# A mixture-of-experts decoder layer: routed products weighted and scattered to token order by each tile, instead of gathered per token at the end

## The chip, the cores and the metric

The kernel runs on one core of a Trainium2 chip. The metric is device time in microseconds, from the first to the last instruction of the core and the little that lies around it; the time of a kernel is the median of its runs. One further execution is taken with the hardware profiler; every line of a profile shown here comes from that execution.

## The reference, cut to what matters

The input is 64 sequences of 128 tokens with 256 channels, float32, 8,192 tokens in all. Each token passes a state-space block, a cross attention, and then this feed-forward block with a residual and a layernorm around it:

```python
shared = (silu(x @ shared_gate.T) * (x @ shared_up.T)) @ shared_down.T
probs = sigmoid(x @ router_w.T + routing_bias)          # 8 experts
scores, indices = top_k(probs, 2)
scores = scores / sum(scores)
w = zeros(tokens, 8); w[token, indices] += scores
g = silu(einsum('th,ehi->tei', x, gate_w))
u = einsum('th,ehi->tei', x, up_w)
combined = einsum('tei,eih,te->th', g * u, down_w, w)
out = layernorm(x + shared + combined)
```

Only the two experts with a weight other than zero need to be computed for a token. So there are 16,384 rows to send through an expert, each 256 floats (1 KB).

## The kernel before, in words

All of it lies in `_shared_decay`. Tokens are handled in `NG` = 16 groups of `GB` = 4 sequences (512 tokens). A group goes through `front`, `scan`, `after` (state space, attention, layernorm; its result is `x2`), then `route`, and then its shared expert, `shared`.

**Routing.** `route` ranks the experts of each token, finds by a prefix sum the row that each of the token's two copies gets in its expert's region of the DRAM array `xs`, writes that row into `index`, and sends the rows of `x2` there with 8 indirect DMAs on POOL (L1024). Then it works out `weight`, the two scores of each token, and keeps it in SBUF.

**Tiles.** `tile_list(k)` turns the counts of the experts into a list of tiles. There are five batches (`BATCHES`): 57 tiles of 256 rows and, in the last batch, 21 of 128 rows. In the last batch the rows behind the end of each expert are filled with zeros (8 indirect DMAs, L1096). `routed` runs over the tiles. `fetch` copies the tile's entry on POOL (L1196), and SP reads it into registers, loads the expert's weights (1.5 MB into one of `NW` = 3 slots, L1199, which waits until the last user of the slot is done) and the rows (L1205, into `rows_in`, 3 buffers). `hidden` transposes the rows on PE (L1219) and makes the gate and up products, ACT applies silu, DVE multiplies. `down` makes the down product, ACT copies it to `rows_out` (2 buffers, L1245), and SP stores it to the DRAM array `ys` in tile order (L1246). The tile loop runs `down(i-1)` after `hidden(i)`, and then fetches ahead.

**The end.** `places` (80 small DVE instructions) changes every entry of `index` from a row of `xs` to a row of `ys`. For the groups 7 to 13 (`LATE`), `x2` has been parked in the DRAM array `x2_rows`, and their shared expert is computed only now (`late_shared`, L1337), interleaved with `combine` of all 16 groups. `combine` gathers the two products of each token from `ys` with 8 indirect DMAs on POOL (`picked`, 12 buffers of 1 KB per partition, L1268), adds them with the weight as a scalar (8 DVE instructions, L1272), makes the layernorm and stores the group. In `layernorm` POOL computes `rstd` (L636), DVE then `shift` (L638), and ACT applies both (L641). `load_rows` (L1074) brings `x2` or `x2` plus shared product back into `x2_back`, 4 buffers.

**What sets the order.** `weave` interleaves generators by shares: in the stage after the groups, `places` along the remaining tiles; at the end, `combine` along `late_shared`. The framework then fixes the queue of each engine before the run, and each engine works its queue strictly in order. A place in the weave is a priority rather than a position. So the 16 steps of `places` were meant for the length of 180 steps of tiles, but the trace has their first and last multiply-compare (L1168) start at 1565.8 and 1614.0 us.

Of the kernel before, what the change touches and what calls it, by code (L numbers as in the profile page):

```python
# [16 lines left out]
P = 128  # L17
# [25 lines left out]
NR = sum(n * r for _, _, n, r in BATCHES)  # L43
# [463 lines left out]
def _shared_decay(ctx, K):  # L507
# [84 lines left out]
    index = const.tile([P, NG * GB, 2], mybir.dt.int32, name="index")  # L592
    weight = const.tile([P, NG * GB, 2], F32, name="weight")

    x2_rows = dram.tile([NG, P, GB * D], F32, name="x2_rows", bufs=1)
    xs = dram.tile([NE * CAP + (NE - 1) * P, D], F32, name="xs", bufs=1)
    ys = dram.tile([NR, D], F32, name="ys", bufs=1)
# [13 lines left out]
    bounds = const.tile([P, NE, len(BATCHES)], F32, name="bounds")  # L611
    moves = const.tile([P, NE, len(BATCHES)], F32, name="moves")
    known = [0]
    weights = []
    for i in range(NW):
# [3 lines left out]
    zeros = const.tile([P, D], F32, name="zeros")  # L619
    nc.vector.memset(zeros, 0.0)  # L620
    nc.sync.dma_start(
        out=xs[NE * CAP :, :].rearrange("(i p) d -> p i d", p=P),
        in_=zeros.unsqueeze(1).to_broadcast([P, NE - 1, D]),
    )
# [227 lines left out]
    def after(g, st):  # L852
# [69 lines left out]
        x2 = ring.tile([P, GB, D], F32, name="x2", bufs=2)  # L922
# [10 lines left out]
        st["x2"] = x2  # L933

    writers = []

    def wrote(g, ins):

        tc.declare_no_dep(ins, group="scatters", reason="other rows")
        for k, (groups, *_) in enumerate(BATCHES):  # L940
            if groups <= g:
                tc.declare_no_dep(ins, group=f"fetches{k}", reason="other rows")
        for group in ("scatters", f"scatters{g}"):
            tc.add_to_no_dep_group(group, ins)
        writers.append((g, ins.name))

    def read(k, ins):

        tc.add_to_no_dep_group(f"fetches{k}", ins)
        for g in range(BATCHES[k][0], NG):  # L950
            tc.declare_no_dep(ins, group=f"scatters{g}", reason="other rows")
        for g, name in writers:
            if g < BATCHES[k][0]:
# [10 lines left out]
    def route(g, st):  # L964
# [44 lines left out]
        here = slice(g * GB, (g + 1) * GB)  # L1009
# [11 lines left out]
        nc.vector.tensor_copy(index[:, here, :], at)  # L1021
        for b in range(GB):
            for k in range(2):
                s = nc.gpsimd.indirect_dma_start(  # L1024
                    out=xs, in_=x2[:, b, :], in_offset=None,
                    out_offset=bass.IndirectOffsetOnAxis(ap=index[:, g * GB + b, k : k + 1], axis=0),
                )
                wrote(g, s.ins)
        yield
# [6 lines left out]
        nc.vector.tensor_tensor(  # L1036
            weight[:, here, :], wk2, tot.unsqueeze(2).to_broadcast([P, GB, 2]), ALU.mult
        )
        if g in LATE:
            nc.sync.dma_start(out=x2_rows[g], in_=x2.rearrange("p b d -> p (b d)"))  # L1040
# [33 lines left out]
    def load_rows(g):  # L1074
        t = late.tile([P, GB, D], F32, name="x2_back", bufs=4)
# [3 lines left out]
    def tile_list(k):  # L1079
# [5 lines left out]
        base = sum(m * r for _, _, m, r in BATCHES[:k])  # L1085
# [3 lines left out]
        if last:  # L1089

            behind = small.tile([P, NE], F32, name="behind", bufs=1)
            nc.vector.tensor_tensor(behind, pn, behind0, ALU.add)
            behind_i = small.tile([P, NE], mybir.dt.int32, name="behind_i", bufs=1)
            nc.vector.tensor_copy(behind_i, behind)
            for e in range(NE):
                s = nc.gpsimd.indirect_dma_start(  # L1096
                    out=xs, in_=zeros, in_offset=None,
                    out_offset=bass.IndirectOffsetOnAxis(ap=behind_i[:, e : e + 1], axis=0),
                )
                wrote(groups - 1, s.ins)  # L1100
# [18 lines left out]

        lo = bounds[:, :, k]  # L1120
        nc.vector.tensor_tensor(lo, d, begin1, ALU.add)
        nc.vector.tensor_scalar(cum2[:, 0, :], cum0, float(size), float(base), ALU.mult, ALU.add)
        nc.vector.tensor_tensor(moves[:, :, k], cum2[:, 0, :], lo, ALU.subtract)
# [30 lines left out]
    def places():  # L1154

        n = NE * len(BATCHES)
        step = small.tile([P, n], F32, name="step", bufs=1)
        flat = moves.rearrange("p e k -> p (e k)")
        nc.vector.tensor_copy(step[:, 0:1], flat[:, 0:1])
        nc.vector.tensor_tensor(step[:, 1:], flat[:, 1:], flat[:, 0 : n - 1], ALU.subtract)  # L1160
        low = bounds.rearrange("p e k -> p (e k)")
        for g in range(NG):
            here = slice(g * GB, (g + 1) * GB)
            m = GB * 2
            was = small.tile([P, m], F32, name="was", bufs=1)
            nc.vector.tensor_copy(was, index[:, here, :].rearrange("p b k -> p (b k)"))
            over = small.tile([P, m, n], F32, name="over", bufs=1)
            nc.vector.tensor_tensor(  # L1168
                over, was.unsqueeze(2).to_broadcast([P, m, n]), low.unsqueeze(1).to_broadcast([P, m, n]), ALU.is_ge
            )  # L1170
            nc.vector.tensor_tensor(over, over, step.unsqueeze(1).to_broadcast([P, m, n]), ALU.mult)
            by = small.tile([P, m], F32, name="by", bufs=1)
            nc.vector.tensor_reduce(by, over, AX.X, ALU.add)
            nc.vector.tensor_tensor(
                index[:, here, :].rearrange("p b k -> p (b k)"), was, by, ALU.add
            )
            yield

    def routed():
# [3 lines left out]
        def shape(i):  # L1183

            row = 0
            for k, (_, first, n, size) in enumerate(BATCHES):
# [344 lines left out]
```

## Time and profile before

| | before |
|---|---|
| time, median of 3 runs (lowest, highest) | 2177.42 us (2176.56, 2180.04) |
| the profiled execution: time, span | 2202.88 us, 2201.2 us |
| PE busy | 1986.6 us, 90% |
| DVE, ACT, POOL busy | 1043.9, 733.6, 433.9 us (47%, 33%, 20%) |
| mean granted TensorE clock | 0.959 |
| moved by DMA | 244.85 MB, 111 GB/s |

The time has four parts. Up to about 60 us the first data come in. Up to about 1560 us the groups pass through, with the first tiles among them. Up to 1947 us the remaining tiles run, and from then on the late shared experts and the sums. The profiled execution is 1.2% longer than the median of the plain runs, so differences within the trace are read against 2202.88 and carried over to 2177.42.

In a list of waits a line names the engine and instruction that waited, after the arrow what ended the wait, and then the total, the count and the longest in us. In a timeline a line has the start and length in us, the engine, the line of the code, and in brackets how long the engine had been idle before. SPq is the queue of SP, from which DMAs are issued. PE records of float32 matmuls come in pairs, so 32 records are 16 matmuls.

### The profile page before, as it was taken

To read this page: it belongs to the slowest core of one execution; us is meant where nothing else is said; L and a number is where in the kernel's file an instruction comes from. 1 tells how busy PE (TensorE), PEld (TensorE's weight loads), DVE (VectorE), ACT (ScalarE), POOL (GpSimd) and SP (SyncE) were. 2 spreads that over 40 slices of the span, in tenths; PEclk is the share of its full clock that TensorE was granted. 3 is DMA by queue.
4 is the path that set the end of the run, shared out by engine and by line. 5 is a ranking of instruction groups with operands and counts; after the bars stand their busy time and mean duration, and the time that the engine had idled before them with its cause. 6 is when DMAs were issued, how large, how long until landed. Compare 5 with 4: busy or idle time off the path is not lost. (4 is left out here: it accounts for less than half of the span.)

```text
span 2201.2 us, 25155 instructions
## 1 busy us (share of the span) xinstructions
PE 1986.6 (90%) x8748; PEld 1436.3 (65%) x8748; DVE 1043.9 (47%) x2557; ACT 733.6 (33%) x1173; POOL 433.9 (20%) x504
## 2 busy tenths in 40 slices
PE   4799999999999999999989898989899998877767
PEld 1555666576676867586767676767678887854434
DVE  3667576665555544545455455444541110124453
ACT  2445344434243343333433434341212211112222
POOL 3022123022020212111111202020300000045671
PEclk9899999999999999999999999999899999988879
DMA  4111114122132423242423333232344557425441
GB/s 126 30 51 57 31 57 136 62 77 87 58 113 65 149 82 121 78 144 80 141 91 130 115 106 106 77 128 100 108 173 162 193 204 248 169 74 185 145 141 50
DMA packets 100888, 244.85 MB, mean 111 GB/s; under 512 B 23184, under 2 KB 68752, under 8 KB 91792
## 3 DMA queue, kind: packets, MB, share of 16 engines
q1 hardware_dynamic: 77968, 188.94, 25.9%
q0 software_dynamic: 17280, 51.40, 7.2%
q10 hardware_dynamic: 5504, 2.81, 0.5%
q8 instruction: 71, 1.16, 0.2%
q14 instruction: 65, 0.53, 0.1%
HBM read 202.48 MB, written 54.79 MB: 117 GB/s over the span
## 5 line engine op out<-in xcount | busy, mean ns | idle before, releaser
L664 PE MATMUL gu<-rows_T,routed_w 128*128 128x256 f32 (+1 forms) x2496 | 510.2, 356 | 6.4 <-DVE x2s L1064 5.5
L664 PEld LDWEIGHTS gu<-rows_T,routed_w 128*128 128x128 f32 x2496 | 420.1, 193 | 75.9 <-issue 16.3
L673 PE MATMUL pm<-routed_w,hid 128*128 128x256 f32 x1080 | 274.7, 401 | 0.0
L1234 DVE TENSOR_TENSOR hid<-hid,gu 128x512 f32<-128x512 f32 x135 | 92.4, 685 | 376.1 <-PE gu L664 361.0
L664 PE MATMUL gu<-x2T,shared_w 128*128 128x512 f32 x512 | 238.1, 610 | 25.8 <-ACT x2T L652 15.5
L664 PE MATMUL pm<-xnT,w_in_s 128*128 128x512 f32 x512 | 245.3, 604 | 0.7 <-ACT xnT L654 0.7
L673 PEld LDWEIGHTS pm<-routed_w,hid 128*128 128x128 f32 x1080 | 210.7, 202 | 31.6 <-issue 4.3
L664 PEld LDWEIGHTS gu<-x2T,shared_w 128*128 128x128 f32 x512 | 96.8, 195 | 144.5 <-issue 106.1
L673 PE MATMUL gu<-shared_w,hc 128*128 128x256 f32 x512 | 136.7, 420 | 43.5 <-DVE hc L1056 21.7
L702 DVE SCALAR_TENSOR_TENSOR xc<-pm,cw,xc 128x508 f32<-128x508 f32 (+2 forms) x192 | 140.3, 739 | 68.7 <-ACT xc L697 65.7
L1233 ACT ACTIVATE hid<-gu 128x512 f32<-128x512 f32 x135 | 80.3, 595 | 270.7 <-PE gu L664 252.2
L1024 POOL DMA_INDIRECT xs<-x,index x128 | 140.7, 1099 | 144.9 <-issue 125.0
L673 PEld LDWEIGHTS gu<-shared_w,hc 128*128 128x128 f32 x512 | 105.4, 212 | 73.4 <-DVE hc L1056 25.0
L1245 ACT COPY rows_out<-pm 128x512 f32<-128x512 f32 (+1 forms) x78 | 41.2, 528 | 334.5 <-PE pm L673 312.7
L664 PEld LDWEIGHTS pm<-xnT,w_in_s 128*128 128x128 f32 x512 | 96.4, 194 | 83.5 <-issue 72.8
L1268 POOL DMA_INDIRECT picked<-ys,index x128 | 125.2, 978 | 104.2 <-DMA ys<-rows_out 26.7
L1196 POOL COPY rows_in<-what 1x3 int32<-1x3 int32 x78 | 14.8, 193 | 583.3 <-PE pm L1219 483.6
L673 PE MATMUL pm<-w_out_s,sz 128*128 128x256 f32 x512 | 114.5, 380 | 1.9 <-DVE sz L848 1.2
L673 PEld LDWEIGHTS pm<-w_out_s,sz 128*128 128x128 f32 x512 | 96.5, 190 | 17.0 <-issue 2.4
L857 POOL DMA_DIRECT2D cT<-in_ctxT_dram x16 | 12.4, 777 | 449.3 <-PE pm L914 255.5
L636 POOL TENSOR_TENSOR rstd<-var,mhalf 128x4 f32<-128x4 f32 x64 | 65.9, 1030 | 166.5 <-DVE var L634 93.4
L697 ACT ACTIVATE xc<-pm,cb,cw 128x512 f32<-128x512 f32 x64 | 49.5, 774 | 119.9 <-PE pm L664 119.9
(225 smaller groups left out, 2611.1 us busy)
## 6 DMA issues: line engine op xcount, KB each, us to landing
routed_w<-in_ffn_dram SPq DMA_DIRECT2D x78, 1536.0 KB
rows_in<-xs SPq DMA_DIRECT2D x57, 256.0 KB
ys<-rows_out SPq DMA_DIRECT2D x57, 256.0 KB
xt<-in_x_dram POOLq DMA_DIRECT2D x16, 512.0 KB
cT<-in_ctxT_dram POOLq DMA_DIRECT2D x16, 512.0 KB
cq<-chunks SPq DMA_DIRECT2D x16, 512.0 KB
x_back<-x_rows SPq DMA_DIRECT2D x16, 512.0 KB
out_dram<-o SPq DMA_DIRECT2D x16, 512.0 KB
```

What stands on the lines that cost most here:

```text
L636: nc.gpsimd.tensor_tensor(rstd, var, mhalf, ALU.pow)
L664: nc.tensor.matmul(ps, lhsT=w[:, k, col : col + P], rhs=src[:, k, :], start=(k == 0), stop=(k == KD - 1),)
L673: nc.tensor.matmul(ps, lhsT=src[k], rhs=w[:, k, cols], start=(k == 0), stop=(k == chunks - 1))
L697: nc.scalar.activation(xcf[:, c, :], ps, AF.Identity, bias=cb[:, c : c + 1], scale=cw[:, c, TAPS - 1 : TAPS],)
L702: nc.vector.scalar_tensor_tensor(xc[:, c, :, s:], ps3[:, :, : L - s], cw[:, c, TAPS - 1 - s : TAPS - s], xc[:, c, :, s:], ALU.mult, ALU.add,)
L857: nc.gpsimd.dma_start(out=cT, in_=ctxT[:, g * T : (g + 1) * T].rearrange("(k p) t -> p k t", p=P))
L1024: s = nc.gpsimd.indirect_dma_start(out=xs, in_=x2[:, b, :], in_offset=None, out_offset=bass.IndirectOffsetOnAxis(ap=index[:, g * GB + b, k ...
L1196: nc.gpsimd.tensor_copy(entry, what[:, i, :])
L1233: nc.scalar.activation(hc, psg, AF.Silu)
L1234: nc.vector.tensor_tensor(hc, hc, psu, ALU.mult)
L1245: nc.scalar.copy(y, ps)
L1268: nc.gpsimd.indirect_dma_start(out=y, out_offset=None, in_=ys, in_offset=bass.IndirectOffsetOnAxis(ap=index[:, s, k : k + 1], axis=0),)
```

## The change

The row of `xs` grows from 256 to 258 floats (`DX`). Behind the 256 channels it carries the row of `ys` to which its product belongs (`slot`, token order, two rows per token) and the token's weight. Each tile reads these two columns with two small POOL copies, ACT scales the product by the weight while it copies it out of PSUM (one instruction per 128 rows in place of one per tile), and POOL scatters 128 rows per indirect DMA to `ys`. So `ys` is in token order, `places` goes, and `combine` becomes one plain load of 1 MB per group on SP, two DVE adds of 128x1024, and the layernorm in place. The rows behind each expert get zeros with a row of `ys` of their own, so that they do not hit a token: the eight indirect scatters and seven stores of these rows form `fill_behind`, each of which raises the row numbers in the one tile `zeros` on DVE first. The buffers `x2_back` go from 4 to 3.

```diff
-NR = sum(n * r for _, _, n, r in BATCHES)
+DX = D + 2
...
-    index = const.tile([P, NG * GB, 2], mybir.dt.int32, name="index")
-    weight = const.tile([P, NG * GB, 2], F32, name="weight")
+    slot = const.tile([P, NG * GB, 2], F32, name="slot")
+    nc.gpsimd.iota(slot, pattern=[[2 * L, NG * GB], [1, 2]], base=0, channel_multiplier=2,
+                   allow_small_or_imprecise_dtypes=True)
...
-    xs = dram.tile([NE * CAP + (NE - 1) * P, D], F32, name="xs", bufs=1)
-    ys = dram.tile([NR, D], F32, name="ys", bufs=1)
+    xs = dram.tile([NE * CAP + (NE - 1) * P, DX], F32, name="xs", bufs=1)
+    ys = dram.tile([2 * 64 * L + (2 * NE - 1) * P, D], F32, name="ys", bufs=1)
...
-    zeros = const.tile([P, D], F32, name="zeros")
+    zeros = const.tile([P, DX], F32, name="zeros")
     nc.vector.memset(zeros, 0.0)
-    nc.sync.dma_start(
-        out=xs[NE * CAP :, :].rearrange("(i p) d -> p i d", p=P),
-        in_=zeros.unsqueeze(1).to_broadcast([P, NE - 1, D]),
-    )
+    nc.gpsimd.iota(zeros[:, D : D + 1], pattern=[[0, 1]], base=2 * 64 * L, channel_multiplier=1,
+                   allow_small_or_imprecise_dtypes=True)
...
-        x2 = ring.tile([P, GB, D], F32, name="x2", bufs=2)
+        row = ring.tile([P, GB, DX], F32, name="x2", bufs=2)
+        x2 = row[:, :, 0:D]
...
+        rows = [st["row"], one.tile([P, GB, DX], F32, name="row1")]
+        nc.scalar.copy(rows[1][:, :, 0:D], x2)
...
-        for b in range(GB):
-            for k in range(2):
-                s = nc.gpsimd.indirect_dma_start(
-                    out=xs, in_=x2[:, b, :], in_offset=None,
-                    out_offset=bass.IndirectOffsetOnAxis(ap=index[:, g * GB + b, k : k + 1], axis=0),
-                )
-                wrote(g, s.ins)
...
+        for k in range(2):
+            nc.vector.tensor_copy(rows[k][:, :, D], slot[:, g * GB : (g + 1) * GB, k])
+            nc.vector.tensor_tensor(rows[k][:, :, D + 1], wk2[:, :, k], tot, ALU.mult)
+        yield
+        for k in range(2):
+            for b in range(GB):
+                s = nc.gpsimd.indirect_dma_start(
+                    out=xs, in_=rows[k][:, b, :], in_offset=None,
+                    out_offset=bass.IndirectOffsetOnAxis(ap=index[:, b, k : k + 1], axis=0),
+                )
+                wrote(g, s.ins)
...
-        t = late.tile([P, GB, D], F32, name="x2_back", bufs=4)
+        t = late.tile([P, GB, D], F32, name="x2_back", bufs=3)
...
-    def places():
...
+    def fill_behind():
+        for j in range(2 * NE - 1):
+            if j:
+                nc.vector.tensor_scalar(
+                    zeros[:, D : D + 1], zeros[:, D : D + 1], float(P), None, ALU.add
+                )
+            if j < NE:
+                s = nc.gpsimd.indirect_dma_start(
+                    out=xs, in_=zeros, in_offset=None,
+                    out_offset=bass.IndirectOffsetOnAxis(ap=behind_i[:, j : j + 1], axis=0),
+                )
+            else:
+                row = NE * CAP + (j - NE) * P
+                s = nc.sync.dma_start(out=xs[row : row + P, :], in_=zeros)
+            wrote(NG, s.ins)
             yield
...
+            to = tiles.tile([P, size // P], mybir.dt.int32, name="to", bufs=3)
+            nc.gpsimd.tensor_copy(to, t[:, :, D])
+            wt = tiles.tile([P, size // P], F32, name="wt", bufs=3)
+            nc.gpsimd.tensor_copy(wt, t[:, :, D + 1])
             yield
...
-            nc.scalar.copy(y, ps)
-            nc.sync.dma_start(out=ys[row : row + size, :].rearrange("(j p) d -> p j d", p=P), in_=y)
+            for j in range(size // P):
+                nc.scalar.activation(y[:, j, :], ps[:, j, :], AF.Copy, scale=wt[:, j : j + 1])
+                s = nc.gpsimd.indirect_dma_start(
+                    out=ys, in_=y[:, j, :], in_offset=None,
+                    out_offset=bass.IndirectOffsetOnAxis(ap=to[:, j : j + 1], axis=0),
+                )
+                tc.declare_no_dep(s.ins, group="products", reason="other rows")
+                tc.add_to_no_dep_group("products", s.ins)
...
-        for b in range(GB):
-            s = g * GB + b
-            for k in range(2):
-                y = late.tile([P, D], F32, name="picked", bufs=12)
-                nc.gpsimd.indirect_dma_start(
-                    out=y, out_offset=None, in_=ys,
-                    in_offset=bass.IndirectOffsetOnAxis(ap=index[:, s, k : k + 1], axis=0),
-                )
-                nc.vector.scalar_tensor_tensor(
-                    x2s[:, b, :], y, weight[:, s, k : k + 1], x2s[:, b, :], ALU.mult, ALU.add
-                )
-            yield
-        o = late.tile([P, GB, D], F32, name="o", bufs=2)
-        yield from layernorm(o, x2s)
-        nc.sync.dma_start(out=out[g * GB : (g + 1) * GB].rearrange("b l d -> l b d"), in_=o)
+        y = late.tile([P, GB, 2, D], F32, name="picked", bufs=3)
+        nc.sync.dma_start(
+            out=y, in_=ys[g * GB * 2 * L : (g + 1) * GB * 2 * L, :].rearrange(
+                "(b p k) d -> p b k d", p=P, k=2)
+        )
+        yield
+        for k in range(2):
+            nc.vector.tensor_tensor(x2s, x2s, y[:, :, k, :], ALU.add)
+        yield
+        yield from layernorm(x2s, x2s)
+        nc.sync.dma_start(out=out[g * GB : (g + 1) * GB].rearrange("b l d -> l b d"), in_=x2s)
+        yield
...
-    weave(rows, 6 * BATCHES[-2][2] + 4 * BATCHES[-1][2], (places(), NG, True))
+    weave(rows, 6 * BATCHES[-2][2] + 4 * BATCHES[-1][2], (fill_behind(), 6 * NE, True))
```

Not shown: the number of the groups that a tile's loads wait for (`needs`) is one higher for the last batch, so that its tiles also wait for `fill_behind`; three DVE instructions per batch go from `tile_list`.

## The prediction

> **What bounds the kernel now.** The page gives PE 90% of the span, so I first cut the span into its stages with the busy times by stretch (window, length, then PE, PEld, DVE, ACT and POOL busy, granted clock, DMA share, GB/s).
>
> ```profile
> 800.00:1560.00 760.00, 712.32 (x3235) 538.03 (x3234) 377.64 (x892) 282.55 (x439) 113.35 (x131) 0.97 0.33 109
> 1600.00:1805.00 205.00, 204.82 (x953) 170.72 (x953) 39.30 (x76) 40.43 (x72) 3.00 (x17) 1.00 0.51 175
> 1805.00:1947.00 142.00, 122.18 (x862) 112.60 (x861) 14.45 (x21) 26.45 (x61) 3.00 (x17) 0.96 0.54 189
> 1947.00:2188.00 241.00, 175.01 (x506) 99.93 (x504) 106.79 (x320) 54.56 (x103) 140.82 (x143) 0.85 0.41 130
> 2188.00:2201.20 13.20, 0.00 (x0) 0.00 (x0) 3.56 (x11) 2.07 (x4) 1.01 (x1) 0.70 0.13 45
> ```
>
> The groups and the 256-row tiles are bound by PE. The 128-row tiles lose 20 us of PE, the last stage 66, and its clock is 0.85. What PE needs there I read from an undisturbed stretch: between the end of two down products (2166.15 and 2187.96) lie 21.8 us, so seven late groups take 152.6. The rest of 254.1 us (1947.1 to 2201.2) is 66 idle, 175.0 - 152.6 = 22.4 slow clock, 13.2 tail. The waits of this stage say who holds PE:
>
> ```profile
> DVE shift L638 <- POOL rstd L636: 59.1, 12, 8.9
> PE gu L673 <- DVE hc L1056: 21.7, 5, 7.1
> PE gu L673 <- issue: 16.0, 3, 11.5
> PE gu L664 <- ACT x2T L652: 15.5, 3, 9.1
> ```
>
> and the timeline shows one such chain:
>
> ```profile
> 1975.42 0.94 POOL L1268 DMA_INDIRECT picked<-ys,index  x1 [0.30 <-issue]
> 1976.38 1.05 POOL L636 TENSOR_TENSOR rstd<-var,mhalf 128x4 f32<-128x4 f32 x1
> 1977.47 0.16 DVE L638 SCALAR_TENSOR_TENSOR shift<-mv,rstd 128x4 f32<-128x4 f32 x1 [8.87 <-POOL rstd L636]
> ...
> 1979.45 0.67 DVE L1056 TENSOR_TENSOR hc<-hc,gu 128x512 f32<-128x512 f32 x1
> ...
> 1980.17 1.22 PE L673 MATMUL gu<-shared_w,hc 128*128 128x256 f32 x2 [11.46 <-issue]
> ```
>
> `rstd` stands behind ten gathers in POOL's queue, DVE blocks at `shift`, `hc` stands behind that, PE starves. POOL is the root: 128 gathers at 0.96 + 0.30 us are 161 us of its queue.
>
> In the 128-row tiles PE waits for rows:
>
> ```profile
> PE pm L1219 <- DMA rows_in<-xs: 19.8, 10, 3.5
> ```
>
> ```profile
> 1866.09 0.37 ACT L1245 COPY rows_out<-pm 128x256 f32<-128x256 f32 x1 [2.10 <-PE pm L673]
> 1866.49 0.33 SPq L1246 DMA_DIRECT2D ys<-rows_out  x1
> 1867.81 0.33 SPq L1199 DMA_DIRECT2D routed_w<-in_ffn_dram  x1
> ```
>
> SP waits for ACT to store `ys`, reads registers for 1.3 us, and only then issues the next weights, with the rows behind them.
>
> **What the Trainium skill says.** TensorE: Matmul & The Clock Gate, Part 1, has the clock at half after an idle window of about 3.4 us. The trace agrees: 0.50 in 1580 to 1585, after an idle of 5.5. So each idle us costs another 22.4/66 = 0.34. DMA: Bandwidth & Descriptors, "Anatomy of one DMA", prices a DMA from POOL at 2.0 us plus its bytes at 436 GB/s; here a gather issued at 1950.35 was used at 1953.11, 2.76 us. The same page, "Issuing engines are not separate DMA queues": a store moved from SP to POOL saves no transfer. GPSIMD Engine Reference, Key points: POOL contends with DVE instructions that have two SBUF inputs. The trace has one `lg` multiply at 1.22 us against 0.16 while POOL multiplies `cj`, but none of that while it issues scatters (L811 keeps 1.22 between 1156 and 1158), so 135 more scatters don't slow DVE.
>
> **The change, part by part** (profiled time, 2202.88 us, span 2201.2).
>
> *Last stage.* POOL loses 161 us and keeps 16 `rstd` of 1.04. DVE: 8 x 0.48 = 3.8 us per group become 2 x 1.22 (128x1024 adds, as L811) = 2.4. SP gets 16 loads of 1 MB, as many bytes as the gathers: about 32 MB in all, in 190 us 170 GB/s, against 329 in the busiest 5 us seen (1595 to 1600), so DMA doesn't bind. What idle remains is an estimate:
> - The first load of `ys` waits on SP until the last scatter has landed (later loads of `x2_back` queue behind it, the first is in already). Three such loads, 3 MB, then take some 10 us, and their adds stand before `hc` on DVE: 5 us.
> - `x2_back` has 3 buffers and the sums now hold one until their store has landed. At the first border the second late group's load waits for such a release: 4 us (one load takes 4.42). Later borders are covered, as two sums fit into one late group of 21.8 us.
> - ACT applies a layernorm in one block of 2.07 us ahead of the silu of `hc`, about once per late group beyond slack: 8 us.
>
> That is 17 idle, 6 clock. The tail grows: both adds now follow the last shared product, instead of half of the eight; 2.4 against 1.7, and the statistics of all four sequences instead of two (+1.1): 15.0. Sum 152.6 + 17 + 6 + 15 = 190.6 against 254.1: **-63.5**.
>
> *128-row tiles.* No store stands on SP. Its 1.8 us from the end of the down product to the weights (1866.01 to 1867.81) go; the register reads run while SP would wait. The loop of two tiles (1860.27 to 1874.73, 14.46 us) becomes 12.7, against 10.9 that PE needs; the idle of 19.8 halves: **-9**. POOL's entry copy (L1196) is now behind a scatter (1.26), but it runs a tile ahead.
>
> *fill_behind.* 15 rounds, each a DVE add that waits until the DMA before it has landed, since both use one tile. By price a POOL round is 0.17 + 1.0 + 2.8 = 4 us; a round on SP queues behind 1.5 MB of weights, 3 to 7. The framework pulls such work forward (`places` was done by 1615), so the adds stand among `hid` multiplies on DVE. Some 65 us of rounds, of which the queue order planned perhaps two thirds; a slack of 6 us per tile (the PSUM slot of DVE's multiply is wanted 6.5 us later) takes most. Bounds 0 and 25: **+8**. The 29 us of `places` on DVE and three instructions per batch go: 0, DVE had been idle under PE; so with the 8 old scatters on POOL.
>
> *Groups.* Per tile: two POOL copies (0.2 each) and two scatters (1.26), 41 tiles, 120 us on a queue busy 252 of 1500. Per group ACT copies 128x1024 (1.06, as L795), DVE adds four small instructions (0.17), the scatters leave 1 to 2 us later, with a batch's fetch a group away. ACT's two scaled copies take about 0.94 instead of 0.59 (L835 is 0.1 dearer than a plain copy); they now wait for a POOL copy of the weight, with silus behind them on ACT, but that copy is due when the tile's rows land, a tile earlier. `rows_out` comes free when the scatters have landed, 2 x 1.26 + 2.8 = 5.3 us on, against two tiles of 11 us. All hidden under PE at 94%; if the cover is gone, the place is `rstd` behind two scatters, 2.5 us. Bounds -3 and +20: **+3**.
>
> *Start.* The 896 KB of zeros ahead of the first `xt` go, 2.8 us at 329 GB/s, less two iotas on POOL (0.15 each, as L601; `slot` is larger): **-1.5**.
>
> *Rows of 1032 bytes*: 0.8% more bytes for `xs`, hidden behind PE; 0, at worst 1 us per 128-row tile if the odd length halves the rate of the 128 KB (bounds 0 to 15, inside the range).
>
> Sum -63.5 - 9 + 8 + 3 - 1.5 = -63. The profiled execution should take 2140; carried to the median, 2177.4 - 63 x 0.988 = **2115 us**.
>
> **The rivals.**
> *The loads become serial.* SP's queue holds stores that wait for ACT, and `x2_back` is released late at all six borders: add, issue, 4.4 us load, transposes, copy, about 6 us each beyond now. Idle 17 - 4 + 36 = 49, clock 17, stage 233.6, gain 20.5; sum -20, **2158**. For it: SP waits 155.8 us for `o` after 1600. Against: the plain loads no longer hang on POOL.
> *Everything hidden.* Idle 6 in the last stage (174, -80), the 128-row tiles lose only 5 (-15), zeros -2.8, groups and fill 0: -98, **2081**.
> *POOL becomes the bound in the groups (slower).* If a scatter waiting for ACT stands before `rstd`, the POOL time of 120 us reaches PE. From 66 of them (55%) on the gain is gone; at 70%, **2198**. Against: no wait of PE in the groups names POOL, and it is 83% idle there.
>
> **How the numbers follow.** Likeliest 0.62 (2095 to 2138), serial 0.17, all hidden 0.13, slower 0.05, and 0.03 for a mix that ends within 0.2%, about what a measurement of this kernel can tell from no change. Faster 0.92. Leaving out 0.05 to 0.1 on either side, the range runs from near the all-hidden case to just past the serial one: 2084 to 2160.
>
> **What would show it.** In the last stage PE idle under 25 us, clock over 0.93, `shift` waiting for `rstd` about 16 x 1.2 us; 128-row tiles with `rows_in` waits near 10; `fill_behind`'s adds on DVE with waits for DMAs around 1570 to 1640; the waits at L1005 in the groups as before. Wrong would be: PE at the transposes waiting for `x_back`, or `shift` waiting longer in the groups.

## The result, and the profile after

The changed kernel takes **2163.78 us** (median of 4 runs, 2159.85 to 2164.41) against 2178.65 us of the kernel before beside it (2176.56 to 2180.04): a ratio of 0.9929, 95% interval 0.9912 to 0.9946, 15 us faster. The forecast was 2115, range 2084 to 2160. Its profiled execution took 2163.97 us (span 2162.1); that of the kernel before had taken 2202.88. So the two traces differ by 39 us, of which the forecast had 63.

The stages of the kernel after, cut as before (window, length, then PE, PEld, DVE, ACT and POOL busy, granted clock, DMA share, GB/s). The last tile's product is copied out at 1970.6 us:

```profile
800.00:1560.00 760.00, 708.77 (x3184) 531.70 (x3184) 382.01 (x896) 295.00 (x472) 182.23 (x242) 0.97 0.32 106
1600.00:1805.00 205.00, 191.31 (x858) 157.80 (x857) 27.70 (x52) 40.05 (x79) 46.27 (x87) 0.97 0.49 169
1805.00:1947.00 142.00, 127.05 (x858) 113.73 (x857) 15.35 (x23) 31.08 (x66) 31.88 (x81) 1.00 0.64 222
1970.00:2148.00 178.00, 160.97 (x506) 93.80 (x504) 91.38 (x222) 54.89 (x103) 19.01 (x17) 0.95 0.52 179
2148.00:2162.10 14.10, 0.00 (x0) 0.00 (x0) 4.81 (x13) 2.07 (x4) 1.01 (x1) 0.58 0.13 42
```

The last stage idles 17 us of PE where it idled 66, and its clock is 0.95 for 0.85. But 1600 to 1805, full before (204.82), has lost 13.5 us, and the stage starts 23 us later. Five events, the same in every kernel here, show where: the last counting matmul of `route`, the last sum of an early shared expert, the last tile's copy out of PSUM, the last sum of a late shared expert, the end.

| us | last count | early sum | last tile | late sum | end |
|---|---|---|---|---|---|
| before | 1557.0 | 1624.5 | 1947.4 | 2188.0 | 2201.2 |
| after | 1585.4 | 1657.9 | 1970.6 | 2147.6 | 2162.1 |
| gained or lost between | +28.4 | +5.0 | -10.2 | -63.6 | +1.3 |

Nearly all of the missing 24 us is lost before the last group is routed. The list of DVE's waits over the whole run has three lines that the kernel before doesn't have:

```profile
DVE row L1035 <- DMA xs<-row,index: 59.5, 15, 7.1
DVE zeros L1152 <- DMA xs<-zeros,behind_i: 32.9, 8, 8.5
DVE zeros L1152 <- DMA xs<-zeros: 14.8, 6, 5.4
```

The second and third are the chain of `fill_behind`, which was forecast. The first wasn't. L1035 writes `slot` into column 256 of the rows, and for the second copy, `row1`, there is one buffer. The timeline in the first group, whose counting matmul was at 132.4 us:

```profile
144.68 0.68 DVE L1063 TENSOR_TENSOR hc<-hc,gu 128x512 f32<-128x512 f32 x1
...
149.75 0.96 POOL L1040 DMA_INDIRECT xs<-row,index  x1 [0.30 <-issue]
152.49 0.17 DVE L1035 COPY row<-slot 128x4 f32<-128x4 f32 x1 [7.13 <-DMA xs<-row,index]
152.59 0.69 DVE L826 TENSOR_TENSOR mt<-mt,pm 128x512 f32<-128x512 f32 x1
153.43 5.44 PE L840 MATMUL pm<-mt,xd 128*128 128x128 f32 x32 [6.25 <-DVE mt L826]
```

The copy at 152.49 belongs to the *next* group, whose counting matmul comes at 213.9, 61 us later. It reads only the constant `slot`, so nothing but the buffer holds it, and the framework put it into DVE's queue right behind the current group's work. There it waits for the last of this group's scatters out of `row1`, issued at 149.75, to land: 2.74 us after the issue. An estimate by the Trainium skill's price for these 132 KB (DMA: Bandwidth & Descriptors, "Anatomy of one DMA", 2.0 us plus bytes at 436 GB/s) is 2.3 us; the trace is a little above it. Behind it stands `mt` of the scan, and PE idles 6.25 us. PE's waits up to 1553 us show it as an item of its own (the kernel before has 43.1, nothing and 2.0 us in these three lines):

```profile
PE pm L1009 <- DVE sel L999: 47.5, 11, 7.0
...
PE pm L840 <- DVE mt L826: 11.1, 3, 6.2
PE pm L1202 <- DMA rows_in<-xs: 5.5, 1, 5.5
```

The chain of `fill_behind`, in the timeline:

```profile
1605.64 0.15 DVE L1152 TENSOR_SCALAR zeros<-zeros 128x1 f32<-128x1 f32 x1 [8.51 <-DMA xs<-zeros,behind_i]
1605.72 0.69 DVE L1221 TENSOR_TENSOR hid<-hid,gu 128x512 f32<-128x512 f32 x1
1606.07 0.96 POOL L1156 DMA_INDIRECT xs<-zeros,behind_i  x1 [1.83 <-DVE zeros L1152]
1606.46 2.08 PE L672 MATMUL gu<-shared_w,hc 128*128 128x256 f32 x4 [4.89 <-DVE hid L1221]
```

A tile's `hid` multiply stands behind the add, and PE behind it. And the last stage, DVE's and then PE's waits (from 1947 and from 1970 us):

```profile
DVE shift L637 <- POOL rstd L635: 16.0, 16, 1.2
```

```profile
PE gu L663 <- ACT x2T L651: 5.6, 5, 3.5
PE pm L649 <- DMA x_back<-x_rows: 5.0, 2, 2.7
PE gu L672 <- DVE hc L1063: 4.5, 3, 2.3
```

### The profile page after: what moved, and what is told of

It is laid out like the page before. It is cut to its first block, busy times and chain, and to the rows that moved or that the text cites. A ratio compares the mean times of both kernels' runs of the same rounds, so it can differ in the third digit from the quotient of the medians.

```text
span 2162.1 us, 25066 instructions
## 1 busy us (share of the span) xinstructions
PE 1974.3 (91%) x8748; PEld 1428.0 (66%) x8748; DVE 1008.4 (47%) x2426; ACT 767.2 (35%) x1248; POOL 468.7 (22%) x669
## 4 chain that ended last, share of the span: by engine, by line
PE 64%; DVE 6%; DMA 5%; ACT 4%; issue 3%; POOL 2%; SPq 0%; ACTq 0%; DVEq 0%; POOLq 0%
PE gu L663 22%; PE pm L672 17%; PE pm L663 12%; PE gu L672 2%; DMA rows_in<-xs 2%; PE pm L717 2%; PE pm L840 2%; PE pm L649 1%; PE pm L1202 1%; PE pm L913 1%; PE pm L927 1%; DMA xs<-zeros 1%; PE pm L833 1%; POOL xs L1040 1%; DMA x_back<-x_rows 1%
## 5 line engine op out<-in xcount | busy, mean ns | idle before, releaser
L663 PE MATMUL gu<-rows_T,routed_w 128*128 128x256 f32 (+1 forms) x2496 | 505.1, 353 | 0.7 <-ACT rows_T L1204 0.7
L663 PEld LDWEIGHTS gu<-rows_T,routed_w 128*128 128x128 f32 x2496 | 415.0, 190 | 69.9 <-issue 15.8
L1234 POOL DMA_INDIRECT ys<-rows_out,to x135 | 134.0, 993 | 503.7 <-ACT rows_out L1233 432.1
L1233 ACT ACTIVATE rows_out<-pm,wt 128x256 f32<-128x256 f32 x135 | 57.8, 471 | 341.9 <-PE pm L672 328.3
L672 PE MATMUL gu<-shared_w,hc 128*128 128x256 f32 x512 | 125.7, 395 | 12.9 <-DVE hc L1063 8.0
L672 PEld LDWEIGHTS gu<-shared_w,hc 128*128 128x128 f32 x512 | 99.0, 198 | 38.7 <-DVE hc L1063 10.9
L1040 POOL DMA_INDIRECT xs<-x,index x64 | 68.9, 1076 | 143.8 <-DVE row L1036 70.0
L640 ACT ACTIVATE x<-x,shift,rstd 128x256 f32<-128x256 f32 x128 | 67.6, 590 | 53.2 <-DVE shift L637 53.1
L1204 ACT COPY rows_T<-pm 128x512 f32<-128x512 f32 (+1 forms) x78 | 41.2, 528 | 117.3 <-PE pm L1202 117.2
```

Of the source, the lines that this page charges most:

```text
L640: nc.scalar.activation(dst[:, b, :], src[:, b, :], AF.Identity, bias=shift[:, b : b + 1], scale=rstd[:, b : b + 1])
L663: nc.tensor.matmul(ps, lhsT=w[:, k, col : col + P], rhs=src[:, k, :], start=(k == 0), stop=(k == KD - 1),)
L672: nc.tensor.matmul(ps, lhsT=src[k], rhs=w[:, k, cols], start=(k == 0), stop=(k == chunks - 1))
L1040: s = nc.gpsimd.indirect_dma_start(out=xs, in_=rows[k][:, b, :], in_offset=None, out_offset=bass.IndirectOffsetOnAxis(ap=index[:, b, k : k ...
L1233: nc.scalar.activation(y[:, j, :], ps[:, j, :], AF.Copy, scale=wt[:, j : j + 1])
L1234: s = nc.gpsimd.indirect_dma_start(out=ys, in_=y[:, j, :], in_offset=None, out_offset=bass.IndirectOffsetOnAxis(ap=to[:, j : j + 1], axis=0),)
```

## Experiments

All times are medians; `r` is the ratio to the kernel before on the same chip, with its 95% interval. The kernel before itself stands at 2178 to 2181 us in two sets of runs and at 2196 to 2199 in four (last part below), so ratios are compared rather than times across sets.

### The groups: the copy of the places

```diff
-            nc.vector.tensor_copy(rows[k][:, :, D], slot[:, g * GB : (g + 1) * GB, k])
+            nc.vector.scalar_tensor_tensor(
+                rows[k][:, :, D], tot, 0.0, slot[:, g * GB : (g + 1) * GB, k], ALU.mult, ALU.add
+            )
```

> Changed kernel with one edit: the copy of the places into the second copy's column 256 also reads the normaliser of the weights (times 0), so DVE can't have it in its queue before this group's own weights are there. Same number of instructions, same result. Theory (the copy, drawn forward on DVE, waits for the previous group's scatters to land and holds up DVE): DVE's 59.5 us of waits for those DMAs fall under 3, the last group's counting matmul moves from 1585 us back to 1557 to 1562, and the time falls by 20 to 28 us, to 2136 to 2144. Rival (the cause is POOL's added scatters or ACT's row copy in the groups): the time stays within 0.2% of the changed kernel's 2163.8 us and PE's waits in the groups move to another releaser.

Measured: 2146.39 us, r 0.9755 (0.9734 to 0.9777). DVE has no wait at `row` left. The line of the counting matmul, after and here (its last start ahead of the semicolon):

```profile
L1009 PE MATMUL pm<-sel,upto x32: 193/297/423, 132.4 to 1585.4; 128*128 128x32 f32 x32
```

```profile
L1009 PE MATMUL pm<-sel,upto x32: 192/297/423, 130.7 to 1566.3; 128*128 128x32 f32 x32
```

Against the changed kernel run once more (2164.52, in another set), a copy that waits for its own group's weights gives back 18 us, and 19 of the 28 in the trace. The theory holds, with 2 us less than the least expected, and the last count stands 4 us past its range; 9 us of the groups stay.

### The fill: windows in place of a raised tile

```diff
-    zeros = const.tile([P, DX], F32, name="zeros")
+    zeros = const.tile([P, DX + 2 * NE - 2], F32, name="zeros")
...
-    nc.gpsimd.iota(zeros[:, D : D + 1], pattern=[[0, 1]], base=2 * 64 * L, channel_multiplier=1,
+    nc.gpsimd.iota(zeros[:, D:], pattern=[[P, 2 * NE]], base=2 * 64 * L, channel_multiplier=1,
...
-            if j:
-                nc.vector.tensor_scalar(
-                    zeros[:, D : D + 1], zeros[:, D : D + 1], float(P), None, ALU.add
-                )
...
-                    out=xs, in_=zeros, in_offset=None,
+                    out=xs, in_=zeros[:, j : j + DX], in_offset=None,
```

> Changed kernel with one edit: the 15 stores of filling rows read 15 overlapping windows of one tile (each window has its own row number in column 256), so no DVE add stands between two of them. The filling rows hold other finite numbers than zeros, the result is the same. Theory (the chain of add and landed DMA holds DVE in the stretch 1600 to 1660): the 47.7 us of DVE waits at the add go, PE is busy 200 us or more of 1600 to 1805 instead of 191, and the time falls by 8 to 20 us, to 2144 to 2156. Rival (the cost is the traffic of the 15 stores, or the chain was covered): 2160 to 2167.

> Both edits. Theory: the two waits lie in different stretches and add up, 2118 to 2134, near the 2115 forecast. Rival (one stretch waits for the other, or the waits were covered): 2140 or more.

Measured: 2159.21 us alone (r 0.9814, 0.9798 to 0.9829) and 2139.34 with both edits (r 0.9727, 0.9710 to 0.9744). Beside the first edit the second gives 7 us in plain runs. From the last count to the early sum it is 64.8 and 64.9 us with windows, alone and with both, against 72.5 to 73.5 with the chain: 8 us. So in these runs, which stand beside a kernel before of 2198.69, the chain costs what it was priced at; the last part shows that this holds for such sets only. Alone the windows end 3 us above their range, with both edits 5 us, and PE is busy 198 us of 1600 to 1805 where 200 or more were expected: the chain is worth the low end of what was expected.

### The other 9 us of the groups

With both edits the groups run even with the kernel before up to the fourth, are 5.7 us late at the fifth, and 9.7 at the last. These are differences of single traces: seven profiles with the groups of the kernel before have the last count at 1551.5 to 1557.0 us, and seven with this edit of the copy, the yield kept, have it at 1563.6 to 1568.7, some 12 us later on average. Three candidates were taken out one at a time. First, ACT's copy of the rows is held until the weights are there:

```diff
-        nc.scalar.copy(rows[1][:, :, 0:D], x2)
...
+        nil = ad[:, 0, 0:1]
+        nc.vector.tensor_scalar(nil, tot[:, 0:1], 0.0, None, ALU.mult)
+        nc.scalar.activation(rows[1][:, :, 0:D], x2, AF.Identity, bias=nil)
```

> The kernel with both edits (places written late, windows) and one more: ACT's copy of the rows (1.06 us) takes a zero worked out from the weights as its bias, so that it can't stand ahead of the copies of the transposed rows in ACT's queue, which the router's matmul waits for. Theory (the 9 us that the groups still lose are this copy ahead of the router): the last counting matmul moves from 1566.7 to 1558 to 1562 and the time falls by 4 to 9 us from 2139. Rival (they are POOL's scatters or the rows fetched for the first tile): within 2 us of the kernel with both edits.

Measured: 2143.16 us, r 0.9750 (0.9734 to 0.9766), no gain; the last count moves from 1566.7 to 1564.9, 2 us where 5 to 9 were expected. The copy is not the cause. Second, the tiles' products go out by SP again:

```diff
-                s = nc.gpsimd.indirect_dma_start(
-                    out=ys, in_=y[:, j, :], in_offset=None,
-                    out_offset=bass.IndirectOffsetOnAxis(ap=to[:, j : j + 1], axis=0),
-                )
+            row = sum(shape(m)[1] for m in range(i))
+            nc.sync.dma_start(out=ys[row : row + size, :].rearrange("(j p) d -> p j d", p=P), in_=y)
```

> The kernel with both edits, its products stored by SP in the order of the tiles as the kernel before does, not scattered by POOL. It leaves out the order of the tokens, so the sums at the end add wrong rows, and as their loads then depend on fewer tiles, some may run before the last tile; only the stretches up to the last tile are to be compared. Theory: from the last early shared sum to the last tile 320 to 326 us again instead of 312.6 (SP waits for ACT ahead of the next weights); the last counting matmul in the groups stays at 1565 to 1568. Rival (POOL's scatters cost the groups the 9 us): that matmul moves to 1560 or less.

Measured: the last count at 1568.7, so POOL's scatters of products are not the cause either. From the early sum to the last tile it is 323.2 us again, against 312.6 with both edits: the store that waits for ACT in SP's queue is worth 10.6 us, and the scatters on POOL cost nothing that shows. (2132.07 us in all; seven sums ran early, which is not the changed kernel's stage.)

Third, the start of a group's own scatters. In the fourth group, ahead of the first tile, they leave late. POOL's first scatter in the kernel before with another last stage (below; 358.06 in the kernel before's own trace), then with both edits:

```profile
357.23 1.51 POOL L1024 DMA_INDIRECT xs<-x,index  x1 [4.73 <-issue]
```

```profile
364.31 1.09 POOL L1040 DMA_INDIRECT xs<-x,index  x1 [10.54 <-issue]
```

The `yield` between the weights and the scatters was taken out, on top of the buffers of the next part:

```diff
             nc.vector.tensor_tensor(rows[k][:, :, D + 1], wk2[:, :, k], tot, ALU.mult)
-        yield
```

> The kernel with both edits and five buffers for the reloaded rows, and one yield taken out: the scatters of a group follow its weights in the same step of the weaving and no longer in the next. Theory (in the groups the scatters leave some 7 us later than in the kernel before, the first tile's rows come as much later, and that is the 5 us lost at the fifth group): PE's wait for the first tile's rows falls from 4.7 to 2 us, the fifth group's counting matmul comes 3 to 5 us earlier, the time 2122 to 2125. Rival (the delay is the weights themselves, worked out ahead of the scatters): within 2 us of 2127.5.

Measured: 2115.10 us, but with the kernel before at 2180.81: r 0.9705 (0.9692 to 0.9719). The kernel without this edit has 0.9688 (0.9674 to 0.9702) and, run again, 0.9706, both beside a kernel before near 2196. As the last part shows, ratios from the two levels can't be compared; the traces can. The span is 11.7 us shorter, but 10 of these lie behind the last count, where a run of the same set that keeps the `yield` is as short. The last count comes at 1561.7 us, 2 us earlier, and from the fourth count to the fifth it is 90.0 us, for 87.4 without the edit and 83.0 to 85.1 in four profiles with the old groups. So the edit gains little or nothing. The first scatter leaves at 358.2 instead of 362.2 us and the fetch 1.8 us earlier, but PE now waits 6.2 us for the first tile, 2.7 without the edit.

A fourth candidate stands in the trace with both edits and was not taken out:

```profile
384.56 0.19 POOL L1202 CAST to<-rows_in 128x2 int32<-128x2 f32 x1 [9.04 <-DMA rows_in<-xs]
...
387.25 1.05 POOL L633 TENSOR_TENSOR rstd<-var,mhalf 128x4 f32<-128x4 f32 x1
...
388.33 0.16 DVE L635 SCALAR_TENSOR_TENSOR shift<-mv,rstd 128x4 f32<-128x4 f32 x1 [6.47 <-POOL rstd L633]
```

The new copy of the first tile's places blocks POOL until the tile's rows have landed, and the `rstd` of the next layernorm stands behind it; in the kernel before `shift` waits 2.38 us there. These 9 us are placed in part (5 at the first tile) and not explained.

### The last stage: what the gathers cost

The prediction named `rstd` behind the gathers as what held PE. So in the kernel before, with all its gathers, `rstd` of the sums was worked out on DVE (a first guess by a shift, three steps of Newton):

```diff
-        nc.gpsimd.tensor_tensor(rstd, var, mhalf, ALU.pow)
+        nc.vector.tensor_scalar(ri, var.bitcast(mybir.dt.int32), 1, None, ALU.arith_shift_right)
+        nc.vector.tensor_scalar(rstd.bitcast(mybir.dt.int32), ri, -1.0, float(0x5F3759DF), ALU.mult, ALU.add)
+        for _ in range(3):
+            nc.vector.tensor_tensor(sq, rstd, rstd, ALU.mult)
+            nc.vector.tensor_tensor(sq, sq, var, ALU.mult)
+            nc.vector.tensor_scalar(sq, sq, -0.5, 1.5, ALU.mult, ALU.add)
+            nc.vector.tensor_tensor(rstd, rstd, sq, ALU.mult)
```

> Kernel before with one edit: in the sums of the last stage rstd is worked out on DVE by 14 instructions (about 0.17 us each, 2.4 us per group) and no longer by POOL behind the gathers. All else stays, gathers too. Theory (what held PE was DVE waiting for rstd behind gathers): the last stage falls from 254 us to 185 to 200, the time by 50 to 65 us. Rival (128 gathers of 1.26 us pace the stage themselves, 161 us, and DVE then waits for their rows): it falls by 25 us or less.

Measured: 2198.81 us, r 1.0008 (0.9998 to 1.0019). Nothing. The stage up to the last late sum, before and here:

```profile
1947.40:2188.00 240.60, 174.61 (x504) 99.60 (x501) 106.79 (x320) 54.54 (x103) 140.82 (x143) 0.85 0.41 130
```

```profile
1940.40:2178.50 238.10, 173.50 (x504) 99.15 (x501) 130.68 (x530) 55.09 (x103) 124.32 (x128) 0.85 0.42 131
```

`shift` no longer waits for POOL, and PE idles as long. ACT, with the copies and silus of the shared expert behind, waits 61.9 us in that stage for `shift`, as it had before (66.3). POOL, free of `rstd`, still waits 48.7 us for DVE's adds to give back buffers of `picked` (45.4 before). Three kernels then changed the gathers: all 128 as loads by SP, half of them left out, and one load per group as in the changed kernel.

```diff
-                nc.gpsimd.indirect_dma_start(
-                    out=y, out_offset=None, in_=ys,
-                    in_offset=bass.IndirectOffsetOnAxis(ap=index[:, s, k : k + 1], axis=0),
-                )
+                nc.sync.dma_start(out=y, in_=ys[NR - P :, :])
```

> Kernel before with one edit: each of the 128 gathers of the last stage becomes a plain load of 128 KB issued by SP, always of the last 128 rows of the products, so that it waits for the last tile as the gathers do. It leaves out which rows are summed. The eight multiply-adds, their twelve buffers and rstd on POOL stay. Theory A (the gathers in POOL's queue, 161 us of it, set the pace): last stage 185 to 205 us instead of 254, time 2135 to 2155. Theory B (the lock-step of eight small loads and adds per group over DVE, ACT and SP, whichever queue issues them): 235 us or more, time 2180 or more.

> Kernel before with 64 gathers in place of 128: both multiply-adds of a sequence read the row of its first expert. It leaves out the second expert's rows. Theory A (POOL's gathers pace the stage): 80 us of gathers no longer do, last stage 190 to 210. Theory B (lock-step of the queues): 235 or more.

> Kernel before with the changed kernel's sums (one load of 1 MB, two adds, in place), the load always of the last 1024 rows of the products, so that none runs before the last tile. It leaves out the weights and which rows are summed. Theory (the forecast of the last stage holds on its own): last stage 188 to 196 us, time 56 to 66 us under before, 2130 to 2142. Rival (the 176 us of the run with the loads in tile order came from the loads and not from the seven sums that ran early): 180 or less, 2126 or less.

| kernel before with | time, us | r | last tile to end, us |
|---|---|---|---|
| 128 gathers, as it was | 2195.89 | | 253.8 |
| 64 gathers | 2138.03 | 0.9734 (0.9719 to 0.9749) | 195.3 |
| 128 loads of 128 KB by SP | 2122.72 | 0.9670 (0.9653 to 0.9686) | 177.8 |
| 16 loads of 1 MB | 2137.72 | 0.9731 (0.9715 to 0.9746) | 193.1 |

(The first row's last column is from its profile above.) With 128 loads, eight adds per group, twelve buffers and `rstd` on POOL all unchanged, the stage falls by 76 us; PE is at full clock:

```profile
1942.50:2105.40 162.90, 153.85 (x504) 90.15 (x502) 105.63 (x320) 54.57 (x103) 15.86 (x15) 1.00 0.62 192
```

So the gathers set the pace, and `rstd` was only where it surfaced first. What of a gather it is, its 1.26 us in POOL's queue, its landing, or the buffers it waits for, these runs don't separate: a load by SP differs in all three. The last row answers the forecast itself: 58 us less on its own, the last stage 193.1 us for the forecast 190.6. The loads in the order of the tiles, tried first, mixed this with another gain:

```diff
-        for b in range(GB):
-            s = g * GB + b
...
+        y = late.tile([P, GB, 2, D], F32, name="picked", bufs=3)
+        nc.sync.dma_start(
+            out=y, in_=ys[g * GB * 2 * L : (g + 1) * GB * 2 * L, :].rearrange(
+                "(b p k) d -> p b k d", p=P, k=2)
+        )
```

> Kernel before with the last stage of the changed kernel alone: one plain load of 1 MB per group in place of eight gathers, two adds, layernorm in place, three buffers for the reloaded rows. It leaves out the weights and the order of the tokens (the rows are taken as they lie). Theory (the gathers in POOL's queue ahead of rstd cost the last stage some 62 us in plain runs as well as in the profile): the last stage is 188 to 194 us long and the time 2112 to 2122, 56 to 66 us under the kernel before. Rival (part of that gain exists only in the profiled execution of before): 2135 or more.

Measured: 2122.03 us, r 0.9649 (0.9633 to 0.9665), the last stage 176.0 us: seven groups' loads hung only on early tiles and ran before the last one.

### A faster version

In the trace with both edits, PE waits 8.5 us for `x_back` in the last stage. There five buffers replace three, and two for the loads of products the three there:

```diff
-        t = late.tile([P, GB, D], F32, name="x2_back", bufs=3)
+        t = late.tile([P, GB, D], F32, name="x2_back", bufs=5)
...
-        y = late.tile([P, GB, 2, D], F32, name="picked", bufs=3)
+        y = late.tile([P, GB, 2, D], F32, name="picked", bufs=2)
```

> The kernel with both edits and five buffers for the reloaded rows instead of three, two for the loads of the products instead of three. Theory (of the 25 us of the last stage above PE's need the 8.5 us of PE's waits for reloaded rows are the buffers): those waits fall under 3 and the time by 4 to 10 us, to 2129 to 2135. Rival (they are SP's queue, where the loads stand behind those of the products and the stores): within 2 us of 2139.

> The kernel with both edits and five buffers for the reloaded rows, the loads of the products cut into four of 256 KB per group with eight buffers, and eight small adds for two large ones. Theory (small loads let SP's queue alternate and DVE's adds no longer block 1.22 us each; the run with 128 KB loads had a last stage of 178 us against 193 with 1 MB loads): last stage 175 to 178 us instead of 181, time 2121 to 2126. Rival (the buffers had already given what the pieces give): within 2 us of 2127.5.

Measured: **2127.51 us, r 0.9688** (0.9674 to 0.9702), 12 us under the kernel with both edits; PE's wait for `x_back` is gone and the last stage 180.7 us. The loads in pieces, on top of that, give 2119.18 beside a kernel before of 2180.81, r 0.9721 (0.9708 to 0.9734), no better. Its last stage is 179.9 us long, for 180.7. So the buffers had given what the pieces could. Once more, for the comparison of sets:

> The kernel with both edits and five buffers for the reloaded rows once more, so that it stands in a second set. Theory (it gains as much as the kernel without the yield, and the 12 us between the two are the level of the set): 2114 to 2118 us and a ratio near 0.970 where before is near 2180, 2126 to 2129 and 0.969 where it is near 2196. Rival (taking out the yield gained 12 us): 2127 at either level.

Measured: 2129.78, r 0.9706 (0.9687 to 0.9725). The set was at the upper level again, where both readings expected about this, so the run doesn't decide between them; the traces below do. This version computes the whole reference and is 3% faster than the kernel before, where the change as made has 0.7 and 1.3%.

### The two levels of the kernel before

> The changed kernel once more, unedited, beside the others on one chip. Two earlier sets of runs had the kernel before at 2178.7 and at 2198.7 us. Theory (the level of before differs between sets, that of the changed kernel does not, since what differs lies in a stall of the kernel before at 1571 to 1590 us): 2160 to 2166 us whatever before shows. Rival (the whole set moves together): the ratio to before stays 0.993 and the time moves with it.

> The kernel before, unedited, for a second profile of it. Theory (its two levels, 2178 to 2181 and 2196 to 2199 us, differ by the stall at 1571 to 1590 us, which the records of the first profile show and those of the last two runs lack): where this set is at the lower level, PE is busy 39 of 40 us in 1560 to 1600 instead of 31; where it is at the upper, 31 again. Rival: the levels differ elsewhere, and PE is busy 31 us there at the lower level too.

The changed kernel took 2164.52 us again, beside a kernel before of 2196.03: r 0.9866 (0.9846 to 0.9885). So it doesn't move with the level of before, and its gain is 15 or 32 us depending on the set. The second profile of before fell into a set at the upper level (2197.64 us) and shows the stall of the first (18.3 us) again:

```profile
1581.57 0.60 ACT L1233 ACTIVATE hid<-gu 128x512 f32<-128x512 f32 x1 [18.47 <-remote]
```

"remote" means that no event of this core ends the wait. PE is busy 30.9 of 40 us in 1560 to 1600 there, 32.5 in the version with the buffers, but 39.7 in the two versions (no `yield`, pieces) that were run at the lower level, which have no such line. The changed kernel has no such line in its first profile, taken beside a kernel before of 2178.65. In its second, beside 2196.03, it has:

```profile
1605.01 0.15 DVE L1152 TENSOR_SCALAR zeros<-zeros 128x1 f32<-128x1 f32 x1 [6.38 <-DMA xs<-zeros,behind_i]
1605.13 0.69 DVE L1221 TENSOR_TENSOR hid<-hid,gu 128x512 f32<-128x512 f32 x1
1605.21 0.60 ACT L1220 ACTIVATE hid<-gu 128x512 f32<-128x512 f32 x1 [12.33 <-remote]
```

The stall ends while DVE waits for the chain of `fill_behind` anyway, so it costs nothing that shows. From the last count to the early sum:

| us | stall | no stall |
|---|---|---|
| with the chain | 73.5, 73.5 | 72.5 |
| without the chain (windows) | 63.6 to 70.2, six profiles | 53.6, 53.7 |

(In the two profiles of the windows' first set ACT stands 15.6 and 17.0 us at this place, put down to other causes; they are counted under "stall".) In the version with the buffers, at the lower level with one more edit each, all other stretches agree within 4 us between the sets, so there the level is mostly these 10 us. And the chain hides the stall: it costs about 8 us where the stall stands and, by an estimate from this table, 19 where it doesn't. So the changed kernel shows one level. No profile of the kernel before at the lower level was obtained, so that the stall makes its 18 us is likely and not shown; what causes the stall is open.

## Why the prediction was wrong

**Sum in profiled time.** Forecast -63, measured -38.9 (-39.1 by spans). By its terms:

| term | forecast | measured |
|---|---|---|
| groups and start | +3 - 1.5 | +28.4 |
| `fill_behind` | +8 | +5.0; the chain alone 8 beside the stall, 19 without |
| tiles | -9 | -10.2 |
| last stage | -63.5 | -62.3 |

- **Groups: the step that failed.** "DVE adds four small instructions (0.17)", hidden under PE. The forecast priced their length and not their buffer: one of the four writes a single-buffered tile that scatters still read, and a constant source let it be drawn forward. It waited 59.5 us on DVE, of which 19 reached the end. The bound of +20 left room for POOL's queue and not for this. The rival "POOL becomes the bound in the groups" named the right stage with the wrong place: as in the kernel before, PE waits for POOL only at the very start. But a sign named under "Wrong would be" did come: `shift` waits 66.3 us for `rstd` in the groups, for 50.4. With the products stored by SP that is 53.0, and the last count is no earlier, so most of these waits cost nothing that shows. The forecast saw this mechanism in `fill_behind` (a DVE write to the tile that a DMA reads) and did not ask it of the other tile.
- **Groups, second part.** "The scatters leave 1 to 2 us later, with a batch's fetch a group away": in the fourth group 6 to 7 us later, and the first batch's fetch follows them at once. Some 5 us are lost there, 4 more creep in.
- **`fill_behind`**: right in mechanism, 1.5 to 8.5 us per wait and `hid` behind it; right in size only beside the stall. In the set of the result, whose profile has none, it is by that estimate 19 us, inside the bound of 25 and more than twice the +8.
- **128-row tiles**: right in sum. The next weights leave when the down product ends (1858.98, ACT's copy starts at 1859.13), and two tiles take 13.1 us for the forecast 12.7. From the first 128-row tile to the last it is 130.7 us for 139.3, 8.6 less. But the waits for `rows_in` fall only from 19.8 to 14.9 us, where 10 were expected, the longest from 3.5 to 2.2; the rest is PE's busy time, 119.5 to 115.7 us, as the granted clock rises from 0.96 to 1.00, which the term did not count. That the two add up to 9 is luck. Putting the store back costs 10.6.
- **Last stage**: right in size, idle 17 as forecast, `shift` waits 16 times, 16.0 us in all for the forecast 19. The gathers hold as the root, whether by their time in POOL's queue or not; the path from there to PE was wrong: freeing `rstd` alone gains nothing. PE waits 5.0 us for `x_back` at the transposes, for 4 forecast. More buffers for it, tried on top of both edits, give 12 us, for 9 forecast in borders and first loads.
- **Carrying over to the median.** 2140 became 2115 by the ratio of 0.988. But the profile of before has the stall of the upper level and its median is of the lower, while the changed kernel has one level: its profiled 2163.97 is its median. The 25 us between profile and median were no scale. Most of them are likely the stall, which the chain of `fill_behind` hides in the changed kernel, so that in plain runs that term is dearer than the table's +5.0. This error is as large as that of the groups, and the two together are the 49 us.

## What to carry to other kernels

For every small write that a change adds, ask which buffer it writes, who still reads that buffer, and what else than the buffer holds the write back: without a data dependence it can be queued far ahead and block its engine until a DMA has landed. Here, tying it to a value of its own step cost nothing. And a wait named in a profile is a place where a pace shows, not always its cause; before a profile's sum is carried to a median, see whether both are of one level. And what a wait costs depends on what else stands still at that time: the same chain cost 8 us beside a stall and 19 without.

## What the runs showed that was not expected

Taking away the longest wait of DVE in a stage gained nothing: with `rstd` on POOL, DVE waited for it (59.1 us); with it on DVE that wait was gone, ACT and POOL waited for DVE as before (61.9 us for 66.3, and 48.7 for 45.4), and the time stayed within 0.2%. With one load of 1 MB per group, PE needs two more buffers of reloaded rows to run as it does with eight loads of 128 KB (last stage 193.1 and 177.8 us in the kernel before; 192.1 and 180.7 in the changed one with three and five buffers). And the kernel before stands at two levels 18 us apart, with a stall of 18 us on ACT at the upper that no event of the core ends, while the changed kernel stays at 2164, since its chain of `fill_behind` covers the stall.
